# First layer of a two-layer kernel: other places for the preparation of a token group, z's SiLU one group later, the norm's root in PSUM, D's term in four column groups

## The chip, the cores and the metric

The kernel runs on one core of a Trainium2 chip. The metric is the time of one execution in device microseconds (us); smaller is better. Five engines run side by side, each taking its own instructions in its own order: TensorE (PE, with its weight loads shown as PEld), VectorE (DVE), ScalarE (ACT), GpSimd (POOL), and SyncE (SP), which here only issues DMAs. They wait for each other through semaphores.

## The reference

Two layers are added to an image x of shape (4, 384, 64, 64), each behind a group norm. The change touches only the first layer, a state-space layer over L = 4096 tokens of 384 channels for each of the 4 images:

```python
mu = jnp.mean(xs, axis=-1, keepdims=True)
var = jnp.mean((xs - mu) ** 2, axis=-1, keepdims=True)
xn = (xs - mu) * jax.lax.rsqrt(var + 1e-05) * ln_w + ln_b
xz = jnp.einsum('blc,dc->bld', xn, in_proj_w)        # 768 channels of xb, 768 of z
xc = silu(causal_conv4(xb) + conv_b)
dt, Bm, Cm = split(xc @ x_proj_w.T)
dt = softplus(dt @ dt_w.T + dt_b)
h = exp(dt * A) * h + (dt * xc) * Bm                  # 16 states for each of 768 channels
y = (h * Cm).sum(states) + xc * D
out = (y * silu(z)) @ out_proj_w.T
```

The second layer (windowed attention over 3x3 pixels, with a fold) runs after it and is not changed.

## The kernel before

**Groups of tokens and units.** The tokens of each image are cut into 17 groups ("chunks") of 241, 68 in all. A chunk's recurrence is done in 12 units; a unit is two blocks of 32 channels x 4 states on the 128 partitions, with its other states along the free axis. The main loop (L830) has one step s for each unit. In step s the engines do, for the unit in question:

- DVE: `s_inputs2` of unit s+1 (half of dt·x·B, one 128x964 multiply), then `s_scan` of unit s (two scans of 128x968).
- ACT: `s_decay` of unit s+1: four 128x241 exponentials into buffer da0 once the first scan of unit s has released it, four into da1 after the second scan. So ACT has two gaps in a step into which other work is put, and whatever stands there delays the next group of exponentials, which the next scan needs.
- POOL: `s_outputs` of unit s-1 (h·C, 128x1928), then `s_inputs` of unit s+2 (the other half of dt·x·B, 128x964).
- PE, in every odd step: `s_sum` of units s-3 and s-2: D's term (`ddiag` with xc), then 16 matmuls with a 128x32 weight, which sum the states into y. A `h` buffer (pool `scan`, five of them) is free only after that, and unit s+2 takes the buffer of unit s-3. So in odd steps POOL's `s_inputs` and then DVE's `s_inputs2` wait for y.

**The work beside it.** While one chunk is scanned, the next but one is normalized and the next is prepared, by functions whose names begin with f_. Those of the chunk before (e_) project y to the output. Where each runs is written out by hand: `plan` (L507) and `ends` (L541) are keyed by (r, slot). r is the step counted so that a chunk's own units stand at r = 24 to 35, and the slot is the place within a step: EARLY, READY (both before the scans), SCAN (between ACT's two groups of exponentials), POOL, MID, LATE (after them). `parts` (L569) calls, at each place of step s, what is due for every chunk alive, the youngest first. As the loop repeats every 12 steps, this text gives places as m = r modulo 12; m3 is step 3 of the chunk that is being scanned. Each engine keeps the order in which the code issues (class `InOrder`). The second chunk is prepared while the first is scanned, by the same plan pressed together (`catch_up`, L558).

In order, for a chunk: `f_load`; `f_mean` (three matmuls), `f_center` (DVE), `f_square` (ACT), `f_var`, `f_root`, `f_pow`, `f_rs`, `f_scale` (DVE); `f_x` and `f_z`, each in three parts of six matmuls (`project`) with an eviction by ACT; `f_conv` in three parts of eight matmuls; `f_silu` (ACT loads the SiLU table, works on xc and zs, loads the table of exponential and logarithm again); `f_bc` and `f_xd` (B, C and the rank-24 input of dt); `f_dt` in three parts, `f_plog` and `f_dtx` in three parts each, `f_log`; `f_spread` (eight DMAs that spread B and C over the partitions); `f_b`.

**PSUM.** All of these share a pool of two PSUM tiles (`pmm`, L140). A matmul group that begins waits until the reader of the tile's last contents is done.

**Variance and root.** `f_var` (L305) puts the tokens on partitions: six matmuls of one column each. `f_root` and `f_pow` make rsqrt of a 121x2 tile in SBUF by Ln and Exp; `f_rs` (L326) spreads it over the partitions again, by two matmuls, into a second PSUM tile, which `f_scale` reads.

Of the kernel before, what the change touches and what calls it, by code (L numbers as in the profile page):

```python
# [7 lines left out]
F32 = mybir.dt.float32  # L8
AF = mybir.ActivationFunctionType
# [97 lines left out]
def mamba_layer(ctx, tc, x, w, x1, sc1, bi1, consts, behind):  # L107
# [37 lines left out]
    def load(name, shape, pool=wp):  # L145
        t = pool.tile(shape, F32, tag=name, name=name)
        sp.dma_start(t, w[name])
        return t
# [55 lines left out]
    for i in range(NCB * NX):  # L204
        x_stat(0, i, x_load(0, i))

    onesc = load("onesc", [P, 1], wf)
    lnw = load("lnw", [P, NCB], wf)
    lnb = load("lnb", [P, NCB], wf)
    win = wf.tile([P, NCB, 2 * DI], F32, tag="win", name="win")  # L210
# [93 lines left out]

    def f_var(c):  # L305

        half = (c.t + 1) // 2
        c.spans = [(0, half), (c.t - half, half)]
        pv = pmm.tile([P, 2, TM], F32, tag="mm", name="ps_var")
        for i, (k0, n) in enumerate(c.spans):  # L310
            for cb in range(NCB):
                pe.matmul(
                    pv[:n, i, 0:1], c.sq[:, cb, k0 : k0 + n], onesc, start=(cb == 0), stop=(cb == NCB - 1)
                )
        c.pv = pv

    def f_root(c):
        n = c.spans[0][1]
        c.vs = front.tile([P, 2], F32, tag="vs", name="vs")
        ae.activation(c.vs[:n, :], c.pv[:n, :, 0], AF.Ln, bias=eps[:n, :])  # L320

    def f_pow(c):
        n = c.spans[0][1]
        ae.activation(c.vs[:n, :], c.vs[:n, :], AF.Exp, scale=-0.5)

    def f_rs(c):  # L326
        c.ps = pmm.tile([P, 2, TM], F32, tag="mm", name="ps_rs")
        for i, (k0, n) in enumerate(c.spans):
            pe.matmul(
                c.ps[:, 0, k0 : k0 + n],  # L330
                c.vs[:n, i : i + 1].to_broadcast([n, P]),
                ident[:n, :n],
                start=True,
                stop=True,
            )

    def f_scale(c):
        t, u = c.t, c.u
# [62 lines left out]
    def silu(c, name):  # L401
        g = getattr(c, name)
        ae.activation(g[:, :, 1:], g[:, :, 1:], AF.Silu)
        if c.ci == 0:
            gp.memset(g[:, :, 0:1], 0.0)

    def f_silu(c, *names):
        for name in names:
            silu(c, name)
        ae.preload_act_table_set(EXP_LN)  # L410
        if c.ci > 0:
            for name in names:
                ae.copy(getattr(c, name)[:, :, 0:1], getattr(c.last, name)[:, :, TM:])

    def f_bc(c):

# [83 lines left out]
    def at(f, *args):  # L500
        def part(c):
            f(c, *args)

        part.f = f
        return part

    plan = {  # L507
        (-12, SCAN): [f_load],
        (-11, LATE): [f_mean],
        (-9, READY): [f_center],  # L510
        (-9, SCAN): [f_square],
        (-7, READY): [f_var],
        (-7, SCAN): [f_root],
        (-6, READY): [f_pow],
        (-6, POOL): [f_rs],
        (-5, POOL): [f_scale],
        (7, LATE): [at(f_x, 0)],
        (8, EARLY): [at(f_z, 0)],
        (8, MID): [at(f_x, 1)],
        (9, LATE): [at(f_conv, 0)],  # L520
        (10, SCAN): [at(f_z, 1)],
        (10, POOL): [at(f_z, 2)],
        (11, LATE): [at(f_x, 2)],
        (13, READY): [at(f_conv, 1)],
        (13, SCAN): [at(f_conv, 2)],
        (13, POOL): [at(f_silu, "xc", "zs")],
        (14, EARLY): [f_bc],
        (15, SCAN): [f_xd],
        (16, SCAN): [at(f_dt, 0), at(f_dt, 1)],
        (16, LATE): [at(f_dt, 2)],  # L530
        (17, READY): [at(f_plog, 0)],
        (17, POOL): [at(f_dtx, 0)],
        (18, EARLY): [at(f_plog, 1)],
        (18, READY): [at(f_plog, 2), at(f_dtx, 1)],
        (18, POOL): [at(f_dtx, 2)],
        (19, SCAN): [f_spread],
        (19, MID): [f_log],
        (22, SCAN): [f_b],
    }

    ends = {  # L541
        (-12, LATE): [lambda c: e_load(c)],
        (4, READY): [lambda c: e_project(c, 0)],
        (6, EARLY): [lambda c: e_project(c, 1)],
        (6, SCAN): [lambda c: e_project(c, 2)],
        (7, READY): [lambda c: e_mean(c)],
        (7, LATE): [lambda c: e_store(c)],
    }

# [8 lines left out]
    def catch_up(s, when):  # L558
        for r, w in sorted(plan):
            n = 6 * r + w  # L560
            if 0 <= n < 6 * 20 and ((n - 40) * 23 // 41 if n < 81 else 23 + (n - 81) * 22 // 36) == 6 * s + when:
                for part in plan[r, w]:
                    f = getattr(part, "f", None)
                    if f is f_silu:
                        silu(first, "zs")
                    if f is not f_x:
                        part(second)

    def parts(s, when):  # L569
# [108 lines left out]
    def s_sum(u, u2):  # L678

        c, t = u.c, u.t  # L680
        if u.j % 2 == 0:
            c.y = py.tile([P, 2, TM], F32, tag="y", name="y")
        y = c.y[:, u.j % 2]
        pe.matmul(y[:, :t], ddiag[:, u.j, :], c.xc[:, u.j, :TM], start=True, stop=False, skip_group_check=True)
        for g in range(NG):
            for i in range(4):
                h4 = (u, u2)[i // 2].h4
                pe.matmul(
                    y[CG * i : CG * (i + 1), :t],
                    ssum,  # L690
                    h4[:, i % 2, g, :TM],
                    start=False,
                    stop=(g == NG - 1),
                    skip_group_check=True,
                )
# [12 lines left out]
    def e_load(c):  # L708
        c.lo = 1 if c.ci == 0 else 0
        c.xr = io.tile([P, NCB, XT], F32, tag="xr", name="xr")  # L710
        sp.dma_start(c.xr[:, :, c.lo : TM], e_tokens(c, x))
# [63 lines left out]
    w_bias(2, 3)  # L775
    f_root(first)
    f_pow(first)
    f_rs(first)
    w_bias(3, NJ)
    f_scale(first)  # L780
    w_scale(0)
# [12 lines left out]
    f_root(second)  # L794
    f_pow(second)
    f_x(first, 2)
    f_rs(second)
    f_scale(second)
    f_conv(first, 1)
    f_mean(third)  # L800
    f_center(third, io.tile([P, NCB, XT], F32, tag="xr", name="u"))
    f_conv(first, 2)
    f_silu(first, "xc")
    f_square(third)
    w_bias(NJ, 2 * NJ)
    w_scale(1)
# [10 lines left out]
        f_plog(first, jj)  # L817
        f_dtx(first, jj)
    f_log(first)
    f_rs(third)  # L820
    f_scale(third)
    ae.activation(aneg, alog, AF.Exp)
    ve.tensor_scalar_mul(aneg, aneg, -1.0)
# [476 lines left out]
def layouts(inputs):  # L1300

    import numpy as np

    g = {k: np.asarray(v) for k, v in inputs.items()}
    c = np.ascontiguousarray

    def inner(v):
        v = v.reshape(NJ, P, *v.shape[1:])
        return c(np.swapaxes(v, 0, 1))

    a = {}
    a["x"] = c(g["x"])
    a["lnw"] = c(g["L0_conv_ln_w"].reshape(P, NCB))
    a["lnb"] = c(g["L0_conv_ln_b"].reshape(P, NCB))
    a["win"] = c(g["L0_conv_in_proj_w"].T.reshape(P, NCB, 2 * DI))
    a["cw"] = inner(g["L0_conv_conv_w"].reshape(DI, KC))
    a["cbias"] = inner(g["L0_conv_conv_b"])
    wx = g["L0_conv_x_proj_w"]
    full = lambda v, lo, hi: np.concatenate(
        [np.zeros((lo, v.shape[1]), v.dtype), v, np.zeros((hi - lo - v.shape[0], v.shape[1]), v.dtype)], 0  # L1320
    )
    a["wx"] = inner(c(full(np.concatenate([wx[RK:], wx[:RK]], 0), 0, P).T))
    a["wdt"] = full(np.concatenate([g["L0_conv_dt_w"].T, g["L0_conv_dt_b"][None]], 0), 2 * NS, P)
    a["alog"] = c(
        g["L0_conv_A_log"].reshape(NQ, CG, NG, 4).transpose(3, 1, 0, 2).reshape(P, NQ, NG)
    )
    a["dvec"] = inner(g["L0_conv_D"])
    a["wout"] = c(inner(g["L0_conv_out_proj_w"].T).reshape(P, NJ, P, NCB).transpose(0, 1, 3, 2))

    wa = g["L1_conv_attn_w"].reshape(HEADS * KK, KK, C).swapaxes(0, 1).reshape(-1, C)  # L1330
    a["wa"] = c(wa.T.reshape(P, NCB, -1))
    ab = g["L1_conv_attn_b"].reshape(HEADS * KK, KK).T.reshape(1, -1)
    a["ab"] = c(np.repeat(ab, P, 0))
    a["wv"] = c(g["L1_conv_conv_w"].reshape(KK, C, C).transpose(2, 0, 1).reshape(P, NCB, KK, C))
    wpr = g["L1_conv_proj_w"].T.reshape(NCB, P, P, NCB)
    a["wpr"] = c(wpr.transpose(1, 0, 3, 2))
    a["pb"] = c(g["L1_conv_proj_b"].reshape(P, NCB))
    f = np.float32
    a["ident"] = np.eye(P, dtype=f)
    a["avg"] = np.full((P, P), 1.0 / C, f)  # L1340
    a["blk12"] = np.kron(np.eye(P // 4, dtype=f), np.full((4, 4), 1.0 / 12.0, f)).astype(f)
    a["blk4"] = np.kron(np.eye(P // 4, dtype=f), np.full((4, 4), 0.25, f)).astype(f)
    a["onesc"] = np.full((P, 1), 1.0 / C, f)
    r = np.arange(P)
    k = np.arange(P)
    a["sel"] = c(
        np.stack([(k[:, None] == 4 * i + r[None, :] // CG).astype(f) for i in range(NG // 2)], 1)
    )
    a["own"] = np.repeat(np.eye(GW, dtype=f), KK, 0)
    a["ssum"] = (r[:, None] % CG == np.arange(CG)[None, :]).astype(f)  # L1350
    return a
# [16 lines left out]
```

## Time and profile before

| | us |
|---|---|
| median of three runs (6219.14 to 6224.54) | 6222.57 |
| the profiled execution | 6232.9 |
| its span from first to last instruction | 6231.1 |
| first scan of the loop starts | 112.98 |
| last scan of the loop ends | 4996.8 |
| from 113 to 4997: PE busy | 4264.4 |
| DVE busy | 4645.6 |
| ACT busy | 4125.9 |
| POOL busy | 4765.5 |

The profile is that of one execution. In a timeline a line gives the start, the time, the engine, the operation with out<-in and shapes, how many equal instructions were merged, and in brackets how long the engine had been idle and who ended it. One float32 matmul shows as two MATMUL rows, so "x4" is two matmuls. All of the kernel's instructions bear line L49, that of a helper; tile names tell them apart: ps_var, ps_rs, ps_ln are the norm's, ps_in is `f_x` and `f_z`, ps_cv `f_conv`, ps_xd `f_bc`, ps_dt `f_dt`, ps_lg `f_plog`, ps_out `e_project`. "Granted clock" is the share of TensorE's full clock that it was given.

### The profile page before, as it was taken

What the parts mean: (1) busy time and instruction counts of PE and PEld (TensorE: products, weight loads), DVE (VectorE), ACT (ScalarE), POOL (GpSimd) and SP (SyncE); (2) the same over time, 40 slices, a digit from 0 to 9 for tenths busy, and PEclk for the clock granted to TensorE, in tenths of its full rate; (3) what the DMA queues carried; (4) which work ended last, traced back from release to release, by engine and by line L of the source; (5) the groups of instructions that cost most, each with busy time, mean ns of one, the idle gap of its engine ahead of it and who ended that gap; (6) DMA issues with size and microseconds to landing.
All of it is one profiled execution on the core that took longest, in us unless ns stands there. A gap on an engine that the chain in (4) does not pass through costs nothing.

```text
span 6231.1 us, 114471 instructions
## 1 busy us (share of the span) xinstructions
PE 5542.2 (89%) x40458; PEld 4081.3 (65%) x40458; DVE 5280.4 (85%) x4302; ACT 4753.6 (76%) x12454; POOL 5262.7 (84%) x1987
## 2 busy tenths in 40 slices
PE   6888888888888898888888888888888789999999
PEld 5666766666666676666666666666666455555555
DVE  3999999999999999999999999999999954454444
ACT  3888888888888888888888888888888744444544
POOL 3999999999999999999999999999999944333334
PEclk9899999999989899999899999999899899999999
DMA  4455554555545555555555544555444644444544
GB/s 133 130 142 146 148 139 129 136 139 149 147 130 138 141 137 141 142 130 138 141 145 148 137 124 132 138 143 139 127 130 130 174 143 166 168 167 170 172 167 149
DMA packets 649909, 895.01 MB, mean 144 GB/s; under 512 B 138980, under 2 KB 543990, under 8 KB 649206
## 3 DMA queue, kind: packets, MB, share of 16 engines
q1 hardware_dynamic: 649334, 887.70, 50.7%
q8 instruction: 318, 5.21, 0.4%
q14 instruction: 257, 2.11, 0.1%
HBM read 661.60 MB, written 225.70 MB: 142 GB/s over the span
## 4 chain that ended last, share of the span: by engine, by line
DVE 32%; PE 27%; ACT 16%; POOL 8%; issue 6%; DMA 6%; SPq 4%; DVEq 0%; POOLq 0%; ACTq 0%
DVE h L49 29%; ACT da L49 11%; PE psv L49 9%; POOL h L49 8%; SPq L49 4%; PE pso L49 4%; PE ps L49 3%; PE y L49 3%; PE psa L49 3%; DMA dxr<-dxd 2%; PE ps_out L49 2%; ACT dt L49 2%; DMA dtr<-dtd 1%; DVE dtx L49 1%; PE ps_var L49 1%
## 5 line engine op out<-in xcount | busy, mean ns | idle before, releaser
L49 DVE TENSOR_TENSOR_SCAN h<-da,h 128x968 f32<-128x968 f32 x1632 | 3450.8, 2155 | 111.1 <-issue 65.4
L49 POOL TENSOR_TENSOR h<-h,bc 128x1928 f32<-128x1928 f32 x816 | 3230.2, 3959 | 6.2 <-DVE h L49 4.7
L49 ACT ACTIVATE da<-dtr,aneg 128x241 f32<-128x241 f32 x6528 | 2642.0, 451 | 448.0 <-DVE h L49 435.1
L49 POOL TENSOR_TENSOR h<-dxr,bc 128x964 f32<-128x964 f32 x816 | 1626.0, 1993 | 160.0 <-PE y L49 91.3
L49 PE MATMUL ps_in<-u,win 128*128 128x241 f32 x4896 | 1091.4, 373 | 37.4 <-DVE u L49 18.0
L49 PEld LDWEIGHTS ps_in<-u,win 128*128 128x128 f32 x4896 | 913.5, 191 | 195.0 <-DVE u L49 33.0
L49 DVE TENSOR_TENSOR h<-dxr,bp 128x964 f32<-128x964 f32 x816 | 926.5, 1136 | 130.3 <-PE y L49 121.6
L49 POOL TENSOR_TENSOR bd<-ain,own 99x1188 f32<-99x1188 f32 x192 | 413.4, 2181 | 728.7 <-DMA ain<-ad 542.7
L49 PE MATMUL y<-h,ssum 128*32 128x241 f32 x13056 | 848.4, 403 | 32.5 <-POOL h L49 32.5
L49 PE MATMUL ps_cv<-xb,cdiag 128*128 128x241 f32 x3264 | 693.8, 368 | 2.6 <-ACT neg L49 2.3
L49 PEld LDWEIGHTS y<-h,ssum 128*32 128x32 f32 x13056 | 411.6, 118 | 418.8 <-issue 200.2
L49 PEld LDWEIGHTS ps_cv<-xb,cdiag 128*128 128x128 f32 x3264 | 611.2, 189 | 74.7 <-issue 24.8
L49 PE MATMUL ps_xd<-xc,wx 128*128 128x241 f32 x816 | 331.4, 591 | 330.7 <-ACT xc L49 330.7
L49 PE MATMUL psv<-wv,xp 128*128 128x384 f32 x1728 | 591.3, 494 | 7.9 <-DMA xr<-x 7.9
L49 PE MATMUL ps_out<-zs,wout 128*128 128x241 f32 (+1 forms) x2448 | 541.1, 370 | 0.0
L49 ACT ACTIVATE bd<-ain,own 99x324 f32<-99x324 f32 x704 | 334.7, 556 | 264.3 <-PE ps L49 242.3
L49 PEld LDWEIGHTS ps_xd<-xc,wx 128*128 128x128 f32 x816 | 254.6, 322 | 399.0 <-ACT xc L49 356.1
L49 PEld LDWEIGHTS ps_out<-zs,wout 128*128 128x128 f32 x2448 | 475.3, 194 | 39.1
L49 DVE TENSOR_TENSOR fold<-fold,ps 128x192 f32<-128x192 f32 (+1 forms) x768 | 211.2, 303 | 331.6 <-PE ps L49 317.3
L49 PEld LDWEIGHTS psv<-wv,xp 128*128 128x128 f32 x1728 | 322.0, 191 | 232.2 <-issue 18.5
L49 ACT COPY vst<-psv 128x384 f32<-128x384 f32 x279 | 130.9, 470 | 323.2 <-PE psv L49 323.2
L49 PE MATMUL ps_dt<-xd,wdt 128*128 128x241 f32 x816 | 236.1, 418 | 127.8 <-ACT dt L49 92.9
(113 smaller groups left out, 5552.3 us busy)
## 6 DMA issues: line engine op xcount, KB each, us to landing
dxr<-dxd SPq DMA_DIRECT2D x1632, 120.5 KB
dtr<-dtd SPq DMA_DIRECT2D x1632, 120.5 KB
bc<-bcd SPq DMA_DIRECT2D x544, 120.5 KB
vin<-vd SPq DMA_DIRECT2D x384, 148.5 KB
vd<-vst SPq DMA_DIRECT2D x93, 576.0 KB
dxd<-dtx SPq DMA_DIRECT2D x816, 60.2 KB
dtd<-dt SPq DMA_DIRECT2D x272, 180.8 KB
xs<-in_x SPq DMA_DIRECT2D x96, 256.0 KB
```

Of the source, the lines that this page charges most:

```text
L49: made = self.tc.keep_in_program_order(issue(*args, **kwargs))
```

## The change

Five things are done, all in the first layer:

1. **Variance and root.** `f_var` multiplies the squares by the 128x128 matrix `avg` of 1/384, so that the variance stands on all partitions at once (three matmuls of 241 columns). `f_root` and `f_pow` work on that PSUM tile in place (128x241), and `f_scale` reads it there. `f_rs`, the tile `vs` and the load of `onesc` go. The PSUM tile is held from `f_var` to `f_scale`.
2. **z's SiLU.** `f_gates` does SiLU on xc of this chunk and on zs of the chunk before, in one group between two table loads; the last chunk's zs has a group of its own (`f_last`).
3. **D's term** is four matmuls of 32 columns of `ddiag`, one for each group of 32 output partitions.
4. **New places** for nearly all parts of `plan` and `ends`.
5. `e_load` moves from r = 24 to r = 33, six steps ahead of the first `e_project`.

```diff
     def f_var(c):
-        half = (c.t + 1) // 2
-        c.spans = [(0, half), (c.t - half, half)]
-        pv = pmm.tile([P, 2, TM], F32, tag="mm", name="ps_var")
-        for i, (k0, n) in enumerate(c.spans):
-            for cb in range(NCB):
-                pe.matmul(
-                    pv[:n, i, 0:1], c.sq[:, cb, k0 : k0 + n], onesc, start=(cb == 0), stop=(cb == NCB - 1)
-                )
-        c.pv = pv
+        t = c.t
+        c.ps = pmm.tile([P, 2, TM], F32, tag="mm", name="ps_var")
+        for cb in range(NCB):
+            pe.matmul(c.ps[:, 0, :t], avg, c.sq[:, cb, :t], start=(cb == 0), stop=(cb == NCB - 1))
 
     def f_root(c):
-        n = c.spans[0][1]
-        c.vs = front.tile([P, 2], F32, tag="vs", name="vs")
-        ae.activation(c.vs[:n, :], c.pv[:n, :, 0], AF.Ln, bias=eps[:n, :])
+        v = c.ps[:, 0, : c.t]
+        ae.activation(v, v, AF.Ln, bias=eps)
 
     def f_pow(c):
-        n = c.spans[0][1]
-        ae.activation(c.vs[:n, :], c.vs[:n, :], AF.Exp, scale=-0.5)
-
-    def f_rs(c):
...
+        v = c.ps[:, 0, : c.t]
+        ae.activation(v, v, AF.Exp, scale=-0.5)
...
-    def f_silu(c, *names):
-        for name in names:
+    def f_silu(*gates):
+        for c, name in gates:
             silu(c, name)
         ae.preload_act_table_set(EXP_LN)
-        if c.ci > 0:
-            for name in names:
+        for c, name in gates:
+            if c.ci > 0:
                 ae.copy(getattr(c, name)[:, :, 0:1], getattr(c.last, name)[:, :, TM:])
+
+    def f_gates(c):
+        f_silu((c, "xc"), *([(c.last, "zs")] if c.last else []))
+
+    def f_last(c):
+        if c is live.get(len(chunks) - 1):
+            f_silu((c, "zs"))
...
     plan = {
         (-12, SCAN): [f_load],
-        (-11, LATE): [f_mean],
-        (-9, READY): [f_center],
-        (-9, SCAN): [f_square],
+        (-11, POOL): [f_mean],
+        (-9, READY): [f_center, f_square],
         (-7, READY): [f_var],
-        (-7, SCAN): [f_root],
-        (-6, READY): [f_pow],
-        (-6, POOL): [f_rs],
-        (-5, POOL): [f_scale],
+        (-7, SCAN): [f_root, f_pow],
+        (-7, LATE): [f_scale],
         (7, LATE): [at(f_x, 0)],
-        (8, EARLY): [at(f_z, 0)],
-        (8, MID): [at(f_x, 1)],
-        (9, LATE): [at(f_conv, 0)],
+        (9, EARLY): [at(f_z, 0), at(f_x, 1)],
+        (10, EARLY): [at(f_conv, 0)],
         (10, SCAN): [at(f_z, 1)],
-        (10, POOL): [at(f_z, 2)],
-        (11, LATE): [at(f_x, 2)],
-        (13, READY): [at(f_conv, 1)],
+        (11, EARLY): [at(f_z, 2)],
+        (12, EARLY): [at(f_x, 2)],
+        (12, SCAN): [at(f_conv, 1)],
         (13, SCAN): [at(f_conv, 2)],
-        (13, POOL): [at(f_silu, "xc", "zs")],
-        (14, EARLY): [f_bc],
-        (15, SCAN): [f_xd],
-        (16, SCAN): [at(f_dt, 0), at(f_dt, 1)],
+        (13, MID): [f_gates],
+        (15, EARLY): [f_bc],
+        (15, READY): [f_xd],
+        (16, READY): [at(f_dt, 0)],
+        (16, SCAN): [at(f_dt, 1)],
         (16, LATE): [at(f_dt, 2)],
         (17, READY): [at(f_plog, 0)],
-        (17, POOL): [at(f_dtx, 0)],
-        (18, EARLY): [at(f_plog, 1)],
+        (17, MID): [at(f_dtx, 0)],
+        (17, LATE): [at(f_plog, 1)],
         (18, READY): [at(f_plog, 2), at(f_dtx, 1)],
-        (18, POOL): [at(f_dtx, 2)],
-        (19, SCAN): [f_spread],
-        (19, MID): [f_log],
+        (18, SCAN): [at(f_dtx, 2)],
+        (19, POOL): [f_log],
+        (20, SCAN): [f_spread],
         (22, SCAN): [f_b],
+        (25, MID): [f_last],
     }
 
     ends = {
-        (-12, LATE): [lambda c: e_load(c)],
-        (4, READY): [lambda c: e_project(c, 0)],
+        (-3, MID): [lambda c: e_load(c)],
+        (3, LATE): [lambda c: e_project(c, 0)],
         (6, EARLY): [lambda c: e_project(c, 1)],
-        (6, SCAN): [lambda c: e_project(c, 2)],
-        (7, READY): [lambda c: e_mean(c)],
+        (6, POOL): [lambda c: e_project(c, 2)],
+        (7, EARLY): [lambda c: e_mean(c)],
         (7, LATE): [lambda c: e_store(c)],
     }
...
-        pe.matmul(y[:, :t], ddiag[:, u.j, :], c.xc[:, u.j, :TM], start=True, stop=False, skip_group_check=True)
+        for i in range(4):
+            own = slice(CG * i, CG * (i + 1))
+            pe.matmul(
+                y[own, :t], ddiag[:, u.j, own], c.xc[:, u.j, :TM], start=True, stop=False, skip_group_check=True
+            )
```

In `catch_up` and in the code ahead of the loop the calls of `f_rs` are left out, and `first`'s zs goes through SiLU in `second`'s group, behind `second`'s xc instead of ahead of it.

More of the change, by code (lines that the diff above doesn't have):

```diff
@@ L205, in mamba_layer @@
         x_stat(0, i, x_load(0, i))
-    onesc = load("onesc", [P, 1], wf)
     lnw = load("lnw", [P, NCB], wf)
@@ L305, in f_var @@
     def f_var(c):
-        half = (c.t + 1) // 2
-        c.spans = [(0, half), (c.t - half, half)]
-        pv = pmm.tile([P, 2, TM], F32, tag="mm", name="ps_var")
-        for i, (k0, n) in enumerate(c.spans):
-            for cb in range(NCB):
-                pe.matmul(
-                    pv[:n, i, 0:1], c.sq[:, cb, k0 : k0 + n], onesc, start=(cb == 0), stop=(cb == NCB - 1)
-                )
-        c.pv = pv
+        t = c.t
+        c.ps = pmm.tile([P, 2, TM], F32, tag="mm", name="ps_var")
+        for cb in range(NCB):
+            pe.matmul(c.ps[:, 0, :t], avg, c.sq[:, cb, :t], start=(cb == 0), stop=(cb == NCB - 1))
     def f_root(c):
-        n = c.spans[0][1]
-        c.vs = front.tile([P, 2], F32, tag="vs", name="vs")
-        ae.activation(c.vs[:n, :], c.pv[:n, :, 0], AF.Ln, bias=eps[:n, :])
+        v = c.ps[:, 0, : c.t]
+        ae.activation(v, v, AF.Ln, bias=eps)
     def f_pow(c):
-        n = c.spans[0][1]
-        ae.activation(c.vs[:n, :], c.vs[:n, :], AF.Exp, scale=-0.5)
-    def f_rs(c):
[L327 to L335, printed above, removed]
+        v = c.ps[:, 0, : c.t]
+        ae.activation(v, v, AF.Exp, scale=-0.5)
     def f_scale(c):
@@ L562, in catch_up @@
                 for part in plan[r, w]:
[L563 to L566, printed above, removed]
+                    if getattr(part, "f", None) is not f_x:
                         part(second)
@@ L777, in mamba_layer @@
     f_pow(first)
-    f_rs(first)
     w_bias(3, NJ)
@@ L796, in mamba_layer @@
     f_x(first, 2)
-    f_rs(second)
     f_scale(second)
@@ L802, in mamba_layer @@
     f_conv(first, 2)
-    f_silu(first, "xc")
+    f_silu((first, "xc"))
     f_square(third)
@@ L819, in mamba_layer @@
     f_log(first)
-    f_rs(third)
     f_scale(third)
@@ L1342, in layouts @@
     a["blk4"] = np.kron(np.eye(P // 4, dtype=f), np.full((4, 4), 0.25, f)).astype(f)
-    a["onesc"] = np.full((P, 1), 1.0 / C, f)
     r = np.arange(P)
```

## The prediction

> **What bounds the kernel now.** The stage table first: from the first scan (113 us) to the last (4997) POOL is busy 4765.5 of 4884 us, DVE 4645.6. So the loop stands near two walls, and what can be won is the waits of these two. The waits view from 1000 to 4000 us (1006 scans, 24 for a chunk, so 41.9 chunks and 71.57 us for each) has these at the head of its POOL and DVE rows:
>
> ```profile
> DVE h L49 <- PE y L49: 68.3, 39, 3.1
> POOL h L49 <- PE y L49: 40.4, 28, 2.9
> ```
>
> Nearly one such wait in each chunk, always at m5-m6. Then POOL's own floor, from its timeline, between two starts of the same instruction eight steps apart with no idle time between:
>
> ```profile
> 2030.00 3.93 POOL L49 TENSOR_TENSOR h<-h,bc 128x1928 f32<-128x1928 f32 x1
> ...
> 2076.76 3.94 POOL L49 TENSOR_TENSOR h<-h,bc 128x1928 f32<-128x1928 f32 x1
> ```
>
> 46.76 / 8 = 5.845 us a step, 70.14 a chunk: 1.43 below 71.57. DVE next, in the chunk whose m5 is at 2022:
>
> ```profile
> 2011.19 4.24 DVE L49 TENSOR_TENSOR_SCAN h<-da,h 128x968 f32<-128x968 f32 x2 [0.97 <-POOL h L49]
> ...
> 2025.74 0.63 DVE L49 TENSOR_TENSOR dtx<-ps_lg,xc 128x482 f32<-128x482 f32 x1
> 2027.93 1.16 DVE L49 TENSOR_TENSOR h<-dxr,bp 128x964 f32<-128x964 f32 x1 [1.55 <-PE y L49]
> ```
>
> The next chunk's like scan starts at 2082.61, 71.42 later, with a wait of 0.96 before it. So DVE's own work is 71.42 - 1.55 - 0.96 = 68.9 (two bn_stats in it; the average of 1.4 makes 68.5). The 0.96 is named POOL, but ACT's exponentials for that scan ended at 2011.1 too, behind the SiLU block; it stays. Why y is late is in PE's timeline:
>
> ```profile
> 2018.37 1.08 PE L49 MATMUL ps_dt<-xd,wdt 128*128 128x241 f32 x4 [0.20 <-ACT xr L49]
> 2020.87 1.08 PE L49 MATMUL ps_dt<-xd,wdt 128*128 128x241 f32 x4 [1.41 <-ACT dt L49]
> 2021.78 1.73 PE L49 MATMUL ps_var<-onesc,sq 128*121 128x1 f32 x12
> 2023.37 1.15 PE L49 MATMUL y<-xc,ddiag 128*128 128x241 f32 x2
> 2024.45 3.44 PE L49 MATMUL y<-h,ssum 128*32 128x241 f32 x32
> ```
>
> The third dt part waits for its PSUM tile until ACT, behind four exponentials, has read the first; variance and y queue behind it. And y takes 4.5 us, not the 2.27 of 2036.46 to 2038.73, since the clock falls (stretch, PE busy, PEld, DVE, ACT, POOL, granted clock, DMA):
>
> ```profile
> 2019.10:2022.50 3.40, 1.99 (x14) 1.58 (x12) 3.40 (x3) 3.40 (x10) 3.40 (x2) 1.00 0.77 219
> 2022.60:2029.30 6.70, 6.70 (x43) 3.91 (x44) 5.14 (x5) 5.44 (x15) 5.43 (x3) 0.50 0.39 99
> ```
>
> The clock changes on a grid of 3.41 us. Over the whole trace, leaving one-column matmuls out, full-clock stretches of the grid that were followed by half clock had PE busy at most 52%; those that stayed had at least 46%. I use one half. Behind this y, ACT waits too:
>
> ```profile
> 2031.73 0.37 ACT L49 ACTIVATE xr<-ps_out 128x241 f32<-128x241 f32 x1 [3.66 <-PE ps_out L49]
> ```
>
> **The change, part by part** (times are those of this chunk).
>
> *m3 to m5: the stall.* The first output projection moves from m4 READY to m3 LATE; PE runs it at 2014.2-2017.2 already, so ACT evicts it one gap earlier. dt's first part moves ahead of ACT's first exponentials of m4. On PE: dt0 2017.2-18.1, dt1 to 19.0, and ACT reads dt0 at 18.2-18.7, so dt2 follows at 19.0-19.9 without a wait. dt1 is read in the SCAN gap, as now, by 21.1; the variance takes its tile at 21.1. Three matmuls of 241 columns cost 1.4 (row ps_ln, 1.38 to 1.49) where the twelve one-column rows cost 1.33 to 1.73. y: four of 16 column-group matmuls took 1.77/4 = 0.44, so D's term costs 0.44 instead of 0.51, and y 2.2: 22.5 to 24.7. The stretch 2019.1-2022.5 then holds 2.2 us of wide matmuls (now 1.4), so I take full clock. DVE wants y after dtx and the moved scale, at 27.5, POOL at 2022.86 + 3.9 = 26.8. Both waits go, with 2 us of cover; if the clock falls there all the same, y ends at 26.9 and costs POOL 0.1.
>
> *m5 and m6: what is late next.* Ln and Exp on 128x241 in PSUM have no row: not under 0.37 each (xr<-ps_out, PSUM in) and not over 0.66 (ps_lg, twice the columns, PSUM out); I take 0.45, since that row is nearest in columns to da's 0.45. Against 0.25 and 0.19 now, ACT has 0.46 more a chunk, in the gap before its second exponentials, which DVE wants only after dtx, scale, multiply, gate, dtx and a scan: hidden. But scale now stands right behind dtx (2026.3), and Exp ends at 25.65 + 0.9 = 26.55: DVE loses 0.3 (0.1 to 0.7). The second output projection now takes the PSUM tile that scale frees, at 27.5, not the one that root freed. PE is idle from 24.7 to 27.5: over half a stretch in most positions of the grid, so half clock is likely. The projection (2.96 at full clock) ends at 30.5, or 32 to 33.4; behind it on ACT stand the eviction (0.36), the third plog (0.66) and the exponentials (1.62), which DVE wants at 33.9 (dtx) and 35.4 (scan). Full clock: hidden. All at half: 33.4 + 1.1 = 34.5 and 36.1, so 0.6 to 0.9. I take 0.3. The third projection and y at m7 then end by 38.5 at worst; POOL wants y at 38.45.
>
> In sentences apart: the Trainium skill, page "TensorE: Matmul & The Clock Gate", section "What's actually happening", lets the clock fall after an idle window of about 3.4 us. By it this gap of 2.8 us would cost nothing, and DVE's 0.3 would go. The row above fell with PE busy 1.99 of 3.40 us, so the row decides.
>
> *m8 to m1.* z0 and x1 are issued together one step later; x1 keeps its place on ACT, z0's eviction (0.8) moves from 2044.7 to about 2047, and conv0 takes its tile. From there PE is packed: conv0 3.4, z1 2.4, f_b 0.8, z2 2.4, y 2.2, x2 2.6, conv1 and conv2 6.5, all from the rows 2048.64 to 2069.04, then the mean, now ahead of y, 1.3, and y 2.2: 23.8. From 47.5 this ends at 71.3. DVE, 1.4 ahead of now, wants that y at 71.9, and 0.97 more is covered by its wait behind SiLU; POOL at about 73. Hidden, with about 1.5 of cover; this is the thinnest.
>
> *SiLU.* Two SiLU (1.39 each) and two table loads (1.28 each) a chunk, as now; B's and C's matmuls stand between the same two y on PE and wait for xc as now (5.26 us idle). Once, the last zs costs a pair of loads more (2.6 us on ACT, where no other preparation is left): 0 to 1.
>
> *SP.* The eight spread DMAs (3.8 us of issue) move behind the store of dt and the fetch of the next chunk's first unit: now dtr is issued by 2052.05, so B's four go by 54.0 and, with the 2.82 that dxr took to land, are there at 56.8; POOL wants them at 57.3. Cover 0.5; POOL late by 0 to 1 until DVE's lead has grown. `e_load` keeps 35 us of cover. `onesc` was one of the loads at the head: 0.
>
> *Ends.* In the first chunk (88.8 us from scan to scan) POOL waits 9.43 for a y that stands behind the second chunk's xc; the SiLU ahead of it (1.4) and the wait of ps_rs for the root (1.34) go: 3 (0 to 6). Before the loop Ln and Exp cost 0.46 more and ps_rs goes, three times: 0 (-1 to 1.5).
>
> **Sum.** DVE's round: 68.5 + 0.96 + 0.3 + 0.3 = 70.1. POOL's: 70.14. Two engines this close, and uneven chunks, cost a little more than the larger: 70.4. Then 71.57 - 70.4 = 1.17 a chunk; the first and last left out, 66 x 1.17 = 77, and 3 for the first: 80 us. The profiled execution (6232.9) is 10.3 above the median of the runs shown (6222.57), with the same work: 6232.9 - 80 = 6153 profiled, 6143 as a median.
>
> **Rivals.**
> 1. *POOL alone is the wall* (PE stays at full clock in m5, or DVE's lead covers it): 70.14 + 0.05. 66 x 1.38 + 6 = 97: 6125. For it: DVE without bn_stats (last image) is at 69.2. Against: the gap of 2.8 us.
> 2. *The wait moves to the second projection*: always half clock, Exp at the upper bound. DVE 69.46 + 0.7 + 0.9 = 71.1; 66 x 0.5 = 33: 6190 (6170 to 6208). For it: the 3.66 that ACT waits there now.
> 3. *Slower*: the clock falls once a chunk between m7 and conv0. A low period is 6.83 us (2005.5 to 2012.3), which costs the packed 23.8 us 3.4 more; y at m1 is 2.8 late for DVE, 0.97 of it covered: 70.4 + 1.9 = 72.3, 66 x 0.73 = 48 more, less 3: 6268. It decides from some 1.7 us of idle in one stretch; my walk has 1.1 (z's first part done at 41.4, x's second waiting for ACT until 42.5).
> 4. *It doesn't do what it says*: dt2 is not early enough, y stays behind a half clock: 6210 to 6235.
>
> **How the numbers follow.** Forecast 6143 (6132 to 6170): 0.54. Rival 1: 0.15. Rival 2: 0.15. Rival 4: 0.06, split between slight gain and none. Rival 3: 0.10. A measurement can tell 0.2%, 12 us, from no change. Faster 0.54 + 0.15 + 0.15 + 0.01 = 0.85; same 0.05; slower 0.10. The range runs from 6118 (all of 1.43 and 8 at the ends) to 6205, in rival 2.
>
> **What would show it.** Right: DVE's and POOL's waits for y near zero at m5, ps_dt's wait for ACT dt gone, scans 70.2 to 70.6 us a chunk apart, ps_out waiting for DVE u, half clock still at m2 and often at m6. Wrong: waits for y at m1 or m7, ACT waiting over 3 us for ps_out, DVE waiting for ps_lg, POOL for bc's DMA, or PE at half clock between m8 and m1.

## The result

| | before | after |
|---|---|---|
| median (us) | 6220.85 (6204.60 to 6224.54, 4 runs) | 6385.13 (6381.10 to 6396.12, 4 runs) |
| span of the profiled execution | 6231.1 | 6384.7 |
| mean granted clock of TensorE | .924 | .948 |
| first scan of the loop starts, last one ends | 112.98, 4996.8 | 114.42, 5147.4 |
| a chunk, mean of the 67 behind the first | 71.57 | 73.78 |

The ratio is 1.0272, 95% interval 1.0250 to 1.0294: slower, where 6143 was forecast with 6118 to 6205 as its range. Before and behind the loop little moved (1.4 and 3.0 us); the loop is 149 us longer, with POOL's and DVE's work unchanged (POOL is busy 4772.5 us from 113 to 5150, 4765.5 before). So it is waits again, and where they sit is told by the waits view from 1000 to 4000 us (engine, tile, who was waited for: us in total, times, longest). Of after:

```profile
DVE h L49 <- PE y L49: 223.6, 44, 8.1
...
POOL h L49 <- PE y L49: 121.2, 46, 4.9
...
PE ps_ln L49 <- DMA xt<-in_x: 108.2, 31, 5.1
PE ps_out L49 <- DVE u L49: 92.5, 40, 2.8
...
POOL h L49 <- DMA bc<-bcd: 18.8, 20, 1.9
```

The first two rows were there before, at 68.3 and 40.4. But they are other waits now. Sorted by step, DVE waits for y at m6 in 2 chunks (59 before), and at m2 in 66 of 68 chunks (4 before), 338 us over the whole loop; POOL waits for it at m1 in 59. The third row is new and names the cause: the mean's matmuls (tile ps_ln) wait for the tokens (xt) to arrive. One such place in PE's timeline of after (start, time; in brackets the idle time and who ended it):

```profile
2128.84 6.67 PE L49 MATMUL ps_cv<-xb,cdiag 128*128 128x241 f32 x32
2139.38 2.13 PE L49 MATMUL ps_ln<-xt,avs 128*128 128x241 f32 x6 [3.87 <-DMA xt<-in_x]
2141.45 1.03 PE L49 MATMUL y<-xc,ddiag 128*32 128x241 f32 x8
2142.25 2.39 PE L49 MATMUL y<-h,ssum 128*32 128x241 f32 x32
```

The convolution ends at 2135.5, PE stands for 3.87 us in front of the mean, and the y behind it is done at 2144.6. DVE and POOL at the same time:

```profile
2144.68 1.16 DVE L49 TENSOR_TENSOR h<-dxr,bp 128x964 f32<-128x964 f32 x1 [5.96 <-PE y L49]
```

```profile
2144.82 1.98 POOL L49 TENSOR_TENSOR h<-dxr,bc 128x964 f32<-128x964 f32 x1 [3.22 <-PE y L49]
```

DVE's 5.96 is longer than PE's 3.87; one reason is that mean and y also ran slowly. The stretches around the wait, in four steps of the clock's grid (stretch; busy time and count of PE, PEld, DVE, ACT, POOL; granted clock; DMA share; GB/s):

```profile
2133.20:2136.61 3.41, 2.31 (x12) 1.80 (x10) 3.41 (x4) 2.39 (x8) 3.41 (x2) 1.00 0.93 200
2136.61:2140.02 3.41, 0.64 (x3) 0.64 (x4) 2.11 (x2) 3.33 (x10) 3.41 (x2) 1.00 1.05 252
2140.02:2143.43 3.41, 3.41 (x25) 1.70 (x27) 0.00 (x0) 3.38 (x5) 1.58 (x1) 0.50 0.52 118
2143.43:2146.84 3.41, 3.41 (x35) 2.62 (x28) 2.15 (x3) 2.94 (x5) 2.02 (x2) 1.00 0.00 0
```

The stretch with 0.64 us of matmuls is followed by one at half clock, in which nearly all of the mean and much of y fall. Three terms make the delay against the prediction: 3.87 of waiting, 0.83 more for the mean (2.13 where the prediction had 1.3), 0.94 more for y (3.19 from 2141.45 to 2144.64, 2.25 at full clock): 5.64 us.

Why xt is late is in SP's timeline of after. SP issues the DMAs in order, and from 2109.49 to 2139.56 no gap between two rows is above 0.11 us:

```profile
2109.49 2.23 SPq L49 DMA_DIRECT2D dtd<-dt  x4
2111.76 0.84 SPq L49 DMA_DIRECT2D x<-xr  x1
2112.70 3.12 SPq L49 DMA_DIRECT2D dxr<-dxd  x4
2115.93 1.91 SPq L49 DMA_DIRECT2D dtr<-dtd  x4
2117.88 3.74 SPq L49 DMA_DIRECT2D bc<-bcd  x8
2121.66 0.59 SPq L49 DMA_DIRECT2D xr<-in_x  x1
2122.36 2.53 SPq L49 DMA_DIRECT2D dxr<-dxd  x4
2125.00 3.90 SPq L49 DMA_DIRECT2D dtr<-dtd  x4
...
2134.28 0.59 SPq L49 DMA_DIRECT2D xt<-in_x  x1
```

The same stretch of before has neither the spread (bc) nor the load xr ahead of xt:

```profile
2043.24 2.23 SPq L49 DMA_DIRECT2D dtd<-dt  x4
2045.51 0.84 SPq L49 DMA_DIRECT2D x<-xr  x1
2046.45 3.56 SPq L49 DMA_DIRECT2D dxr<-dxd  x4
2050.13 1.91 SPq L49 DMA_DIRECT2D dtr<-dtd  x4
2052.14 2.45 SPq L49 DMA_DIRECT2D dxr<-dxd  x4
2054.70 1.92 SPq L49 DMA_DIRECT2D dtr<-dtd  x4
...
2062.57 0.59 SPq L49 DMA_DIRECT2D xt<-in_x  x1
2063.21 0.62 SPq L49 DMA_DIRECT2D xr<-in_x  x1
```

From the store of dt to the load of xt it is 24.8 us in after and 19.3 in before. The moved loads cost more than the time to issue them, which the merged row at 2125.00 hides: the fourth of these fetches goes out 2.06 us behind the third, at 2128.59, when xr has landed (2128.58, 6.9 us behind its issue at 2121.66). It waits for the semaphore that xr's load signals, since it uses the same one. The waits view of SP from 1000 to 4000 us has this row in after, and none for xr in before:

```profile
SPq L49 <- DMA xr<-in_x: 25.7, 34, 2.0
```

So the spread and `e_load`, moved ahead of xt, hold its issue back, while the mean, moved ahead of y, wants it earlier and makes y wait with it.

**Theory.** The loss is the mean's wait for xt, made by these three moves together; the rest of the change does what was forecast. **Rivals.** The late xt is a matter of bytes in flight and not of the order of issue; or the loss lies in another part (the variance held in PSUM, the places of dt, D's term, z's SiLU).

### The profile page after: what moved, and what is told of

Read it like the earlier page. It is cut to its first block, busy times and chain, and to the rows that moved or that the text cites. A ratio compares the mean times of both kernels' runs of the same rounds, so it can differ in the third digit from the quotient of the medians.

```text
span 6384.7 us, 117815 instructions
## 1 busy us (share of the span) xinstructions
PE 5421.6 (85%) x42226; PEld 3920.1 (61%) x42226; DVE 5279.1 (83%) x4302; ACT 4790.8 (75%) x12456; POOL 5267.2 (82%) x1987
## 5 line engine op out<-in xcount | busy, mean ns | idle before, releaser
L49 PE MATMUL y<-h,ssum 128*32 128x241 f32 x13056 | 869.0, 397 | 165.3 <-POOL h L49 165.3
L49 PEld LDWEIGHTS y<-h,ssum 128*32 128x32 f32 x13056 | 462.6, 119 | 505.1 <-POOL h L49 200.4
L49 PE MATMUL ps_out<-zs,wout 128*128 128x241 f32 (+1 forms) x2448 | 572.9, 386 | 0.0
L49 PEld LDWEIGHTS ps_out<-zs,wout 128*128 128x128 f32 x2448 | 495.7, 203 | 45.5
L49 PE MATMUL ps_ln<-xt,avs 128*128 128x241 f32 x408 | 139.6, 495 | 215.7 <-DMA xt<-in_x 175.1
L49 PE MATMUL ps_dt<-xd,wdt 128*128 128x241 f32 x816 | 218.2, 411 | 115.8 <-ACT xr L49 112.4
L49 PE MATMUL ps_out<-xr,ident 128*128 128x241 f32 (+1 forms) x408 | 145.1, 439 | 181.8 <-DVE u L49 143.6
```

Of the source, the lines that this page charges most:

```text
L49: made = self.tc.keep_in_program_order(issue(*args, **kwargs))
```

## Experiments

Times are medians beside that of the kernel before in the same comparison. "xt" is the time of its issue, counted from the start of the first scan of m8, "mean" the start of the mean's matmuls, both as medians of 28 chunks (18 to 45, counted from 0); "its wait" is how long PE stood idle just before the mean.

| kernel | us | ratio, 95% interval | xt | mean | its wait |
|---|---|---|---|---|---|
| before | 6220.85 to 6230.95 | | 20.25 | 29.33 | 0 |
| after | 6385.13 | 1.0272 (1.0250 to 1.0294) | 26.72 | 32.05 | 3.88 |
| a1: after, mean behind y | 6147.67 | 0.9867 (0.9853 to 0.9882) | 26.88 | 32.46 | 0 |
| a2: after, spread and e_load back | 6146.25 | 0.9865 (0.9850 to 0.9879) | 21.12 | 29.11 | 0 |
| a3: both | 6142.94 | 0.9859 (0.9844 to 0.9874) | 20.75 | 32.19 | 0 |
| b1: before, with only these three | 6484.36 | 1.0414 (1.0395 to 1.0433) | 25.40 | 30.74 | 3.43 |
| e1: after, spread back | 6145.97 | 0.9868 (0.9852 to 0.9885) | 22.23 | 29.10 | 0 |
| e2: after, e_load back | 6188.47 | 0.9939 (0.9924 to 0.9953) | 25.21 | 29.76 | 1.53 |
| d1: before, D's four groups | 6225.06 | 1.0000 (0.9986 to 1.0013) | | | |
| d2: before, variance in PSUM | 6175.26 | 0.9918 (0.9903 to 0.9932) | | | |
| d3: before, places of dt | 6149.29 | 0.9875 (0.9860 to 0.9890) | | | |
| d6: before, d2 and d3 | 6164.20 | 0.9903 (0.9888 to 0.9917) | | | |
| d4: a3, D's term as one | 6142.31 | 0.9869 (0.9854 to 0.9883) | | | |
| d5: a3, z's SiLU back | 6143.21 | 0.9869 (0.9855 to 0.9884) | | | |

### a1_mean_behind_y

```diff
-        (-11, POOL): [f_mean],
+        (-11, LATE): [f_mean],
```

> The changed kernel with one part put back behind y: the mean's matmuls at LATE of m1 instead of POOL. Theory (DMA): after the change the load of xt is issued some 6 us later against the scans, the mean's matmuls wait for it 3.9 us, and y of m1 stands behind them on PE; with the mean behind y, DVE's wait for y at m2 (6.0 us in most chunks) goes, while POOL's wait of about 0.9 us for B's spread stays: some 70.6 to 71.2 us a chunk and 6140 to 6190 us. Rival A (PE is simply too full from m8 to m1): only the mean's own 1.3 to 2.1 us go, 6250 to 6310. Rival B (the price is in the variance held in PSUM or in D's four matmuls): 6370 to 6400.

6147.67: one line takes nearly the whole loss away, and the gain that was forecast appears. xt is issued as late as in after, but the mean now stands behind y, at 32.46, about when xt has landed. POOL's wait for bc is all but gone too (2 chunks), though the spread stands where it does in after; why it went was not tested.

### a2_old_dma_places

```diff
+        (19, SCAN): [f_spread],
-        (20, SCAN): [f_spread],
...
-        (-3, MID): [lambda c: e_load(c)],
+        (-12, LATE): [lambda c: e_load(c)],
```

> The changed kernel with the mean still ahead of y, but the spread of B and C and the load of the residual put back to their places of before (m7 SCAN, and behind the load of xt at m0). Theory (DMA): the load of xt is issued about 4.4 us earlier (eight spread DMAs 3.8, residual 0.6), so that the mean waits 0 to 1 us instead of 3.9, PE stays at full clock and POOL's wait for the spread goes: 6130 to 6200 us. Rival A (PE too full): 6330 to 6390, since PE's work is the same. Rival B (variance or D's term): 6370 to 6400.

6146.25. The mean still stands ahead of y, and waits for nothing, since xt is issued 5.6 us earlier than in after. Either alone, the mean's move or the two DMAs', costs next to nothing, then; only together are they dear.

### a3_both

Both edits of a1 and a2 in one kernel.

> Both put back: the mean behind y, and the spread and the residual's load in their places of before. Theory (DMA): neither wait is left, 70.2 to 70.7 us a chunk, 6125 to 6160 us, below the kernel before (6221). Rival A (PE too full): 6250 to 6310. Rival B: 6340 to 6390.

6142.94; its interval overlaps those of a1 and a2. It shows the rest of the change without the fault. The waits view from 1000 to 4000 us has no row for xt or bc and none of POOL for y. Two of the rows shown of after are left, and a third here is the scale's wait for the root:

```profile
PE ps_out L49 <- DVE u L49: 75.4, 43, 2.5
...
DVE h L49 <- PE y L49: 18.5, 35, 0.8
...
DVE u L49 <- ACT ps_var L49: 8.2, 14, 0.9
```

A chunk lasts 69.8 to 70.2 in most cases (mean 70.20), and from the first scan to the last (114.63 to 4909.86) POOL is busy 4765.4 of 4795.2 us: POOL is the wall, near the 70.14 that the forecast gave it.

### b1_mean_and_dma_alone

The kernel before with the edits of a1 and a2 the other way round, and nothing else of the change.

> The kernel before with three places alone changed as in the change: the mean at m1 ahead of y, the spread at m8, the residual's load at m9. Theory (DMA): y at m1 comes 3 to 5 us late behind a mean that waits for xt, on top of the old stall at m5: 73.5 to 75.5 us a chunk, 6350 to 6480 us. Rivals A and B: 6215 to 6245, since none of the other edits is in it.

6484.36, 4 us above the range. The mean's wait comes with the three moves alone, on top of the old stall at m5. The waits view from 1000 to 4000 us:

```profile
DVE h L49 <- PE y L49: 269.8, 78, 7.3
POOL h L49 <- PE y L49: 185.0, 72, 5.4
...
PE ps_ln L49 <- DMA xt<-in_x: 109.2, 34, 5.3
...
PE ps_dt L49 <- ACT dt L49: 39.6, 40, 1.4
```

Two waits for y a chunk where before had one. In this kernel the clock is at half for 4.1 us a chunk at m1 (0.1 before).

### e1_spread_back

```diff
+        (19, SCAN): [f_spread],
-        (20, SCAN): [f_spread],
```

> The changed kernel with the spread of B and C alone back at m7 SCAN; the residual's load stays at m9, ahead of xt, and the mean ahead of y. Theory (issue order on SP): xt is issued about 3.8 us earlier, so the mean waits 0 to 0.6 us and not 3.9: 6145 to 6200 us. Rival (bytes: the residual's 361 KB that now go just ahead of xt slow the fetches and xt's own landing): the wait stays over 2 us, 6280 to 6370.

6145.97: with the spread at its old place xt goes out at 22.23 and the mean doesn't wait, although xr's 361.5 KB still go ahead of it. The spread's place in the order of issue decides here, and xr's load ahead of xt is not enough by itself. It isn't free either: SP waits for xr to land 22 times here from 1000 to 4000 us (12.5 us in all).

### e2_residual_back

```diff
-        (-3, MID): [lambda c: e_load(c)],
+        (-12, LATE): [lambda c: e_load(c)],
```

> The changed kernel with the residual's load alone back behind xt at m0; the spread stays at m8. Theory (issue order on SP): xt is issued 0.7 us earlier alone, the mean waits some 3 us, y stays at half clock: 6310 to 6380 us. Rival (bytes): 6150 to 6250.

6188.47, far under the 6310 to 6380 of the theory and inside the rival's range. But e1 has shown that the rival's cause alone makes no wait, and the rows tell why its number came out: `e_load` behind xt brings xt's issue forward by 1.51 us, and xt is there 4.55 us after it instead of 5.33 (from the medians; this part can be xr's bytes). Of the 1.51, 0.59 is the issue of xr, and 0.7 is SP's wait for xr to land (median of the same chunks in after), in which the rival has a part. So the mean waits 1.53 instead of 3.88. I had taken the price to be in proportion to the wait. It isn't. PE's timeline of e2:

```profile
2065.56 1.46 PE L49 MATMUL ps_ln<-xt,avs 128*128 128x241 f32 x6 [1.55 <-DMA xt<-in_x]
```

and the stretch of the clock's grid with this wait, and the next:

```profile
2062.70:2066.11 3.41, 1.86 (x10) 1.43 (x9) 3.41 (x3) 2.33 (x8) 3.41 (x3) 1.00 0.95 283
2066.11:2069.52 3.41, 3.08 (x45) 1.70 (x43) 1.39 (x2) 3.39 (x10) 3.41 (x2) 1.00 1.01 230
```

A wait of 1.55 leaves PE busy 1.86 of 3.41 us, and the clock stays full; one of 3.87 leaves 0.64, and it falls. At m1 the clock is at half for 0.5 us a chunk in e2 and 2.78 in after. The three kernels were timed in different comparisons, so each is taken from its own before: after 164.3 us above, e2 39.6 below, a2, whose mean stands at the same place and doesn't wait, 84.7 below. So the last 2.3 us of waiting cost 203.9 us (3.0 a chunk), and the first 1.5 cost 45.1 (0.66 a chunk). Part of those was covered: between a2 and e2 DVE's waiting for y at m2 grows from 81.9 to 151.3 us, POOL's, the wall's, only from 0.4 to 16.6.

After's own chunks say the same. In the 15 of chunks 2 to 65 in which the mean waits less than 2.5 us, the clock is at half behind it in one, and they last 71.3 us (median); in the 31 with 3.5 us or more it is at half in 30, and they last 75.0.

### d2_variance_alone

The kernel before with the new `f_var`, `f_root` and `f_pow` and with:

```diff
-        (-7, SCAN): [f_root],
-        (-6, READY): [f_pow],
-        (-6, POOL): [f_rs],
-        (-5, POOL): [f_scale],
+        (-7, SCAN): [f_root, f_pow],
+        (-7, LATE): [f_scale],
```

> The kernel before with the variance on all partitions in PSUM, its root in place, and scale at LATE of m5; nothing else of the change. Theory (clock): the three wide matmuls keep PE's stretch ahead of y over one half busy, so the clock does not fall at m5 and y there comes 2 us earlier, though the third dt part still waits 1.4 us: 6150 to 6200. Rival (order: what made y late is dt's wait for ACT): the wait for y stays, 6205 to 6245, the upper end if scale now holds back the output projection.

6175.26, in the range of the theory of the clock, but not quite by its way. The third part of dt waits 1.41 us for ACT as before, and the clock falls all the same, but here for one stretch of the grid instead of two:

```profile
2066.06:2069.47 3.41, 1.41 (x6) 0.68 (x4) 3.41 (x3) 3.24 (x11) 3.41 (x1) 1.00 0.45 120
2069.47:2072.88 3.41, 3.17 (x8) 2.71 (x9) 3.41 (x3) 3.29 (x8) 3.41 (x3) 0.50 0.90 247
2072.88:2076.29 3.41, 2.86 (x38) 1.61 (x36) 3.10 (x3) 3.38 (x12) 3.08 (x2) 1.00 0.10 26
```

In the middle one now stand the wide matmuls of the variance, and y, in the third, is at full clock: 2.34 where it took 4.11 (medians at m5).

### d3_dt_places_alone

```diff
-        (15, SCAN): [f_xd],
-        (16, SCAN): [at(f_dt, 0), at(f_dt, 1)],
+        (15, READY): [f_xd],
+        (16, READY): [at(f_dt, 0)],
+        (16, SCAN): [at(f_dt, 1)],
...
-        (4, READY): [lambda c: e_project(c, 0)],
+        (3, LATE): [lambda c: e_project(c, 0)],
```

> The kernel before with dt's first part and xd at READY instead of SCAN and the first output projection at LATE of m3; nothing else. Theory (clock): dt's wait of 1.4 us goes, but the one-column variance leaves PE's stretch ahead of y under one half busy, y still runs at half clock and ends near 26.9 us in the old chunk's time: DVE waits some 0.6 us, POOL 0.1: 6165 to 6205. Rival (order): the wait for y goes whole, 6130 to 6165.

6149.29, in the range of the order of the work. Here y at m5 still takes 4.05, at half clock, but begins early enough. Either cure takes most of the old stall away (DVE waits for y at m6 for 115.0 us in all before, 4.8 in d2, 13.6 in d3), and this one holds nearly all of the gain: 78.8 us beside 6228.05, where a3 has 88.0 beside 6230.95.

### d6_variance_and_dt

The edits of d2 and d3 together.

> The kernel before with both of the cures for the stall at m5: the variance by a wide matrix with root and power in its PSUM tile, and xd, the first part of dt and the first output projection at their new places. Alone they gave 6175.3 and 6149.3. Theory: both remove the same wait, so they don't add; together they leave what the engines' own work sets, POOL's 69.8 a chunk at best: 6138 to 6155, and the version with everything but the mean and the two DMAs (6142.9) has nothing left to explain. Rival: the new wait of the scale for the root (0.2 to 0.5 a chunk where the variance ran alone) stays and is paid on top of what the places give: 6160 to 6180.

6164.20, in the rival's range, but not by its cause: DVE waits for the root only 2.4 us in all. The two don't add, and together they gain less than d3 alone, 61.5 us beside 78.8, each against its own before (the two intervals just touch). Three timelines of d6 show what came in, PE, ACT and DVE:

```profile
2070.63 0.68 PE L49 MATMUL ps_out<-xr,ident 128*128 128x241 f32 x2 [2.78 <-DVE u L49]
2071.14 4.29 PE L49 MATMUL ps_out<-zs,wout 128*128 128x241 f32 x12
```

```profile
2075.47 0.37 ACT L49 ACTIVATE xr<-ps_out 128x241 f32<-128x241 f32 x1 [3.79 <-PE ps_out L49]
```

```profile
2081.14 2.17 DVE L49 TENSOR_TENSOR_SCAN h<-da,h 128x968 f32<-128x968 f32 x1 [0.52 <-ACT da L49]
```

The variance's PSUM tile is held until the scale is done, so the second output projection begins 2.78 later; PE is idle meanwhile, the clock falls, the projection takes 4.29 instead of 2.61, ACT waits for it, and the exponentials behind it reach DVE's scan at m7 late, by 0.5 in 44 chunks. At m9 DVE loses another 32 us over the loop (64 times), each time in front of a scan whose exponentials have just ended. In a3 DVE hardly has either wait (4.8 and 1.4 us). Which of a3's other places spares it (the third projection in POOL's slot, `e_mean` earlier) was not taken apart.

### d1_dterm_alone and d4_both_dterm_back

d1 is the kernel before with D's four column groups alone; d4 is a3 with one matmul again.

> The kernel before with D's term alone in four column groups; nothing else is moved. In the changed kernel y took 2.25 us at full clock against 2.34 before, so each of the six y of a chunk ends about 0.09 us earlier; DVE and POOL wait for y only once a chunk, at m5, where the half clock doubles that to about 0.2. Theory: 0.1 to 0.2 us a chunk, 7 to 14 us in all: 6214 to 6224 beside 6228. Rival A: the four narrow matmuls cost what the trace's other narrow ones cost with their weight loads, and y is no shorter: 6225 to 6235. Rival B: the shorter y moves DVE's start and breaks the pattern of the half clock at m5, where 1.99 of 3.40 us stood close to the edge: 6190 to 6215.

> The version with the mean behind y and the two DMAs at their old places (6142.94), with D's term as one 128-column matmul again. Theory: no engine waits for y there in most chunks, so 0.09 us a y is covered: 6140 to 6152. Rival: y at m1 or m5 stands just in time and every tenth of a microsecond counts twice a chunk: 68 x 0.2 = 14, 6152 to 6160.

6225.06 beside 6225.66, and 6142.31 (0.9869 of its before, where a3 has 0.9859): no difference that can be measured, in either place. A y at full clock does take 2.25 instead of 2.34, so it isn't rival A's price; the 0.09 is covered nearly everywhere, and at m5 of d1 y stays at half clock (3.80). The gain of 7 to 14 that I gave d1 is not there.

### d5_both_zsilu_back

a3 with z's SiLU in its own chunk's group, and no group of its own at the end:

```diff
-        f_silu((c, "xc"), *([(c.last, "zs")] if c.last else []))
+        f_silu((c, "xc"), *([(first, "zs")] if c is second else []), (c, "zs"))
...
-        (25, MID): [f_last],
```

> The version with the mean behind y and the two DMAs at their old places (6142.94), with z's SiLU in its own chunk's group again: the group at m1 then needs the third part of z of the same chunk, which PE computes at m11, two steps earlier. The number of SiLU and of table loads a chunk is unchanged. Theory: z is done long before, so nothing waits: 6136 to 6150; the pair of table loads that the last chunk's group of its own costs goes, up to 3 us on ACT, where it is covered. Rival: ACT's group waits for z's eviction or the zs of two chunks collide in their buffers (a chunk's zs must be read by the projections before the next one's is written), so that m1 is late by some tenths: 68 x 0.3 = 20, 6155 to 6175.

6143.21 beside a3's 6142.94 (0.9869 and 0.9859 of their own before, with overlapping intervals): the later SiLU of z by itself gives and costs nothing that can be measured.

## Why the prediction was wrong

**The step that failed** is "m8 to m1", with its sentence "From 47.5 this ends at 71.3", and the part on SP beside it. The mean was put ahead of y and counted as 1.3 us of work on PE. That its operand comes by a DMA was left out: the time at which xt lands was never set against the new place. The part on SP saw the spread and `e_load` move past "the store of dt and the fetch of the next chunk's first unit", and weighed them by their own deadlines alone (0.5 and 35 us of cover); that xt now stands behind both in the same queue was not asked. By the table it costs xt 4.1 to 4.5 us for the spread (25.21 - 21.12, 26.72 - 22.23) and 1.1 to 1.5 for `e_load`. In place of "Hidden, with about 1.5 of cover" stand, in the place shown, 3.87 of wait and 1.77 by which mean and y took longer, 5.64 in all. The 31 chunks with 3.5 us of wait or more last 75.2 in the mean, 5.0 more than a3's.

The cover was too large even without xt. In a2 and e1, where the mean has next to no wait, DVE still waits for y at m2 in 67 chunks, 1.2 us each (81.9 and 80.1 us in all). It costs little there, since POOL, the wall, hardly waits.

**The other steps.** Rival 3 had y at m1 late with the clock at half, and had it for 6268; its cause did not come: PE does stand idle between m7 and the convolution, for 1.5 us or more (mostly 1.69) in front of x's second part, in 37 of chunks 2 to 65 of after ("some 1.7" was to be enough), but the clock falls there in none. Its price was half the real one (6268 - 6143 = 125 above the forecast, against 242). Among the signs of a wrong forecast, "waits for y at m1", "POOL for bc's DMA" and "half clock between m8 and m1" all came.

*m3 to m5* was right: in a3 dt's third part no longer waits for ACT (the variance, not urgent, does), y is in time at m5, and DVE waits for y at m6 in 3 chunks. d2 and d3 show that each of the two reasons given, full clock and an earlier start, takes most of DVE's wait away by itself. *m5 and m6*: Ln and Exp take 0.42 and 0.36 (0.45 taken), and DVE waits for Exp 0.14 us a chunk (0.3 taken). The second projection does wait for the scale, but in a3 by 1.75 in the mean (75.4 / 43) and mostly at full clock; "half clock is likely" was wrong there (0.64 us a chunk at m6), and right in the place shown of d6, where rival 2's mechanism came, at a lower price (6164, not 6170 to 6208).

In d6 the 2.78 of wait halved the clock with PE busy 1.21 of that stretch of 3.41 us. The rule of the Trainium skill, page "TensorE: Matmul & The Clock Gate", section "What's actually happening", which lets it fall after an idle window of about 3.4 us, doesn't cover this fall, nor after's with 0.64 busy; e2's stretch with 1.86 busy kept the clock.

*D's term* makes a y 0.09 shorter (0.07 taken), and *SiLU* costs nothing, both without effect on the time. *Ends* was wrong in sign: the first chunk, -3 by the forecast, went from 88.8 to 89.5 in after and 91.8 in a3, where POOL's two waits at m3 and m5 are 11.4 and 7.9 (5.9 and 9.4 before): 1.5 went at m5, and 5.5 came at m3.

**The sum** is near the kernel without the fault: 70.4 a chunk forecast, 70.20 measured in a3, which is what rival 1 has (70.14 + 0.05, POOL alone the wall); a gain of 80 us forecast, 88.0 measured beside a3's own before. That the times agree to 0.1 us (6143 and 6142.94) is luck: in that comparison before took 6230.95, 8 more than the 6222.57 of the forecast. So the mechanism of the gain was right, and what was left out cost nearly three times the gain: 6385.13 - 6142.94 = 242 us, or 252 with each counted from its own before.

## What to carry to other kernels

When an instruction is moved ahead of another on an in-order engine, look up when each of its operands arrives, those that come by DMA too: whoever stands behind it takes over its wait. When a DMA is moved forward in a queue, the ones it passes are what the move costs, and each of them has a deadline of its own. Where each single undoing cures most of the loss, as here, no one move is at fault but their meeting, and making just these moves on the old kernel shows it.

## What the runs showed of the hardware

- The price of a wait on PE is not in proportion to it: beside a2, 1.53 us of wait cost 0.66 a chunk and 3.88 cost 3.66 (each against its own before, over 68), since the longer one also halves the clock for what follows. In the stretches of 3.41 us named here, 0.64, 1.21 and 1.41 of matmuls let it fall, and 1.86 kept it. The row of the prediction that fell with 1.99 has 1.4 without the one-column matmuls.
- One-column matmuls didn't bring the clock back. In before, d1 and b1, which have them, 118 stretches of the grid at half clock had PE busy for over 95%, but under 75% without them: none was followed by full clock. Of those in before with 90% or more without them, 129 of 131 were. In d1 the clock is at half for 10.24 us (2090.74 to 2100.98), over dt's last part, the variance and y, whose median at m5 is 3.80; with the wide ones (d2) the clock was back for y.
- xt, one DMA of 361.5 KB that SP issues in 0.59 us, was there 4.0 to 5.3 us after its issue began (e2's place shown and after's median). Four fetches of dtr mostly take SP 1.9 us to issue, and 3.90 at 2125.00 in after, with SP's wait for xr to land in it (xr, as large as xt, took 6.9 us from its issue).
- With next to no wait for y left, a step of a3 takes 5.85 us in the mean (70.20 / 12), the 5.845 that the prediction read as POOL's floor; the many chunks of 69.8 are a little under it (5.82).
